# Local attention layers of a two-block network: keys copied by ScalarE, output products placed behind another tile's scores

## Chip, cores and metric

One core of a Trainium2 chip runs the whole kernel. Its engines are TensorE (PE, with weight loads shown as PEld), VectorE (DVE), ScalarE (ACT), GpSimd (POOL) and SyncE (SP, which issues transfers). The metric is device time in microseconds, median of several executions. Each engine works through its own list of instructions in a fixed order and waits on semaphores for the others.

## What is computed

Input: 4 sequences of 1024 tokens with 128 features. Block 0 is an attention of softmaxed features and a mixture of experts; block 1 begins with a windowed attention. Its last part, two local-attention layers with an MLP each, is the part that the change touches:

```python
def _layer(x, wqkv, qs, ksc, wo, lg, lb, w1, b1, w2, b2):
    h = shift_token(x)
    q, k, v = jnp.split(h @ wqkv, 3, axis=-1)
    q, k, v = (to_heads(q), to_heads(k), to_heads(v))      # 8 heads of 64
    q = l2norm(q) * qs
    k = l2norm(k) * ksc
    q, k = rotary_xpos(q, k)
    o = local_attention(q, k, v)     # windows of 64 tokens, each sees itself and the one before
    x = x + o.transpose(0, 2, 1, 3).reshape(b, n, INNER) @ wo
    h = shift_token(x)
    h = (h - mu) / jnp.sqrt(var + 1e-05) * lg + lb
    a, g = jnp.split(h @ w1 + b1, 2, axis=-1)
    x = x + (a * jax.nn.gelu(g, approximate=False)) @ w2 + b2
    return x

for l in range(DEPTH):               # DEPTH = 2
    x = _layer(x, ...)
```

All of it is in float32.

## The kernel before

The local layers work on tiles of 128 tokens: 2 layers x 4 sequences x 8 tiles = 64 tiles, counted by g. One loop (from line 1064) walks over g and issues in each iteration the steps of several tiles, so that their chains overlap:

- `scores(g)` (lines 875 to 896): 32 products on 64x64 parts of the array, in two banks of PSUM. VectorE adds the mask and takes the extreme of each row (L892, eight times).
- `project(g + 2, w)` (lines 647 to 676): the queries (w = 0) or keys (w = 1) of the tile two further on. PE multiplies (L653). ScalarE squares (L656, `sq`). VectorE multiplies with the cosine and sine tables (L658 `co`, L663 `si`) and sums the squares (L665, `ss`); `co` waits for `sq`. POOL adds `co` and `si` (L673), for the keys also raises the sums to the power -1/2 (L668, L669) and weights the keys with them (L675).
- `flip(g - 2, j)` (921 to 929): transposes half of the heads' probabilities, which ScalarE copies out (L928, `pt`).
- `over_sums(g - 1)` (907 to 919): VectorE takes the reciprocals of the sums (L912, `sm`); POOL weights half of the heads with them (L919), VectorE the other half (L919), or ScalarE in tiles 3 to 7 of the first sequence (L917, the `light` ones).
- `exps(g)` (898 to 905): eight exponentials on ScalarE (L904), each with its sum.
- `turn(g + 1, w)` (838 to 858): transposes the finished queries or keys. ScalarE copies the queries (L852, `qT`), VectorE the keys (L858, `kT`), which lie in one tile per sequence. In the first tiles the query turn takes twice the products (L849).
- `outputs(g - 3)` (931 to 944): 32 products of probabilities and values, on 128x64 parts of the array; ScalarE copies them out (L944, `os`).
- `values(g - 1)` (860 to 873): one product, a copy by ScalarE (L866, `vs`), and two transfers that SyncE issues and that shift the values by a window (`ve`).
- side steps, listed in `steps`: the output projection of 512 tokens (L951, L952) and the MLP: layernorm in (L972, L144 to L154) and out (L160, L161), gate with GELU (L986, L990), up (L995, L997), down (L1003, L1004).

What sets the order: PE's instructions run in the order in which the loop issues them (`manual_schedule` for PE alone). The lists of ScalarE, VectorE, POOL and SyncE are made by a scheduler when the program is built. It takes, of the instructions that its model holds to be ready, the one that stands first in program order. `issue_after(x)` adds a rule to this: what the block issues on the engine of `x` comes behind `x` in that engine's list. `over_sums` uses it: its VectorE instructions come behind the last `kept["copied"]`, the last copy of keys that had been issued. `kept` and `late` are one dictionary.

PSUM has 8 banks: two for scores, six for all else in the local layers, each given to the next tile when its reader is done.

Of the kernel before, what the change touches and what calls it, by code (L numbers as in the profile page):

```python
# [22 lines left out]
ALU = mybir.AluOpType  # L23
AX = mybir.AxisListType
PSUM = bass.MemoryType.PSUM

P = 128
# [21 lines left out]
def adaln_blocks(ctx: ExitStack, tc: tile.TileContext, a: dict, out: bass.AP):  # L49
    nc = tc.nc  # L50
    pe, act, dve, pool = nc.tensor, nc.scalar, nc.vector, nc.gpsimd
# [11 lines left out]
    def bc(ap, shape):  # L63

        return ap.unsqueeze(len(ap.shape)).to_broadcast(shape)
# [219 lines left out]
    with (  # L285
# [7 lines left out]
        kept = {}  # L293
# [306 lines left out]
    def const1(name, shape):  # L600
        return c1.tile(shape, F32, tag=name, name=name)

    wl = []
    for l in range(DEPTH):
        w = [const1(f"wqkv_{l}", [P, 3, HEADS * DH]), const1(f"wo_{l}", [P, 4, D]), const1(f"w1_{l}", [P, 2 * HID]), const1(f"w2_{l}", [P, 3, D])]
# [38 lines left out]
    late = {}  # L644
    pj = ctx.enter_context(tc.tile_pool(name="pj", bufs=3))

    def project(l, b, t, w, ps):


        nt = f"{l}_{b}_{t}_{w}"  # L650
        if w == 0:
            late[l, b, t, "ss"] = pj.tile([P, 2, HEADS], F32, tag="ss", name=f"ss_{nt}", bufs=4)
        pe.matmul(ps, lhsT=hs[l, b][:, t * P : (t + 1) * P], rhs=wl[l][0][:, w, :], start=True, stop=True)  # L653
        ph = ps.rearrange("p (h e) -> p h e", e=DH)
        sq = pj.tile([P, HEADS, DH], F32, tag="sq", name=f"sq_{nt}", bufs=2)
        act.activation(sq, ph, AF.Square)  # L656
        co = pj.tile([P, HEADS, DH], F32, tag=f"co{w}", name=f"co_{nt}")
        dve.tensor_tensor(co, ph, abs_[l][:, 0, t, w, :].unsqueeze(1).to_broadcast([P, HEADS, DH]), ALU.mult)  # L658
        si = pj.tile([P, HEADS, DH], F32, tag="si", name=f"si_{nt}", bufs=3)

        ex = bass.AP(tensor=ps.tensor, offset=ps.offset + 32, ap=[ps.ap[0], [DH, HEADS], [-32, 2], [1, 32]])
        sn = abs_[l][:, 1, t, w, :].rearrange("p (i e) -> p i e", i=2).unsqueeze(1).to_broadcast([P, HEADS, 2, 32])
        dve.tensor_tensor(si.rearrange("p h (i e) -> p h i e", i=2), ex, sn, ALU.mult)  # L663
        ss = late[l, b, t, "ss"]
        dve.tensor_reduce(ss[:, w, :], sq, AX.X, ALU.add)  # L665
        if w == 1:

            pool.tensor_scalar(ss, ss, 1.0e-24, None, ALU.max)  # L668
            pool.tensor_tensor(ss, ss, nhalf[:, 0:2].unsqueeze(2).to_broadcast([P, 2, HEADS]), ALU.pow)  # L669
        if w == 0 and light(l, b, t):  # L670
            late[l, b, t, "si"] = si
        else:
            pool.tensor_tensor(co, co, si, ALU.add)  # L673
        if w == 1:
            pool.tensor_tensor(co, co, bc(ss[:, 1, :], [P, HEADS, DH]), ALU.mult)  # L675
        late[l, b, t, "co", w] = co

    def light(l, b, t):

        return (l, b) == (0, 0) and t >= EARLY  # L680
# [5 lines left out]
    with (  # L686
# [80 lines left out]
        def project_out(b, k):  # L767
            s = slice(k * BLK, (k + 1) * BLK)
            yp = ps.tile([P, BLK], F32, tag="m", name=f"y1_{b}_{k}")
            pe.matmul(yp, lhsT=wout1, rhs=kept1[b, k, "os"], start=True, stop=True)  # L770
            dve.scalar_tensor_tensor(xT[b][:, s], yp, mods[1][:, 2, b : b + 1], xT[b][:, s], ALU.mult, ALU.add)
# [18 lines left out]
        def when(g, f, *args):  # L790
            if 0 <= g < NG8:
                f(*divmod(g, NT), *args)

        for g in range(-1, NG8 + 2):
            b, t = divmod(g, NT)
            ahead = 0 <= b and b + 1 < B
            if g == -1:
                weights(0, 0)
            when(g + 2, scores)
            when(g + 2, weights)  # L800
            if ahead and t in (2, 4):
                queries(b + 1, t // 2 - 1)
            for after, k, f in ((6, 0, tokens), (8, 0, normed), (11, 1, tokens), (13, 1, normed)):
                if (g - after) % NT == 0 and 0 <= (g - after) // NT < B - 1:
                    f((g - after) // NT, k, "h3")
            for at, k, f in ((1, 0, tokens), (3, 0, normed), (5, 1, tokens), (7, 1, normed)):
                if g == at:
                    f(B - 1, k, "h2")
            when(g - 1, back)
            when(g + 1, flip, (0, 1))  # L810
            when(g + 1, values)
            when(g, outputs)
            when(g + 1, flip, (2, 3))
            if t == 5 and 0 < b <= DEPTH:
                rotary(tab, abs_[b - 1], b - 1)
            if g % 4 == 1 and g > 4:
                project_out((g - 5) // NT, (g - 5) % NT // 4)
            if ahead and t in (3, 5):
                keys(b + 1, t // 2 - 1)

            for i, w in ((0, 0), (0, 1), (1, 0), (1, 1), (2, 0), (2, 1))[max(0, g - NG8 + 6) : max(0, g - NG8 + 7)]:
                project(0, 0, i, w, ps.tile([P, BLK], F32, tag="t", name=f"qk_0_0_{i}_{w}", bufs=2))
# [6 lines left out]
    with (  # L829
# [6 lines left out]
        kept = late  # L836

        def turn(l, b, t, w):
            nt = f"{l}_{b}_{t}_{w}"
            co = kept.pop((l, b, t, "co", w)).rearrange("p h e -> p (h e)")  # L840
            tp = pM.tile([P, 4, P], F32, tag="mid", name=f"qktr_{nt}")
            si = kept.pop((l, b, t, "si"), None) if w == 0 else None
            for i in range(4):
                if si is None:
                    pe.transpose(tp[:, i, :], co[:, i * P : (i + 1) * P], ident)  # L845
                else:

                    for j, x in enumerate((co, si.rearrange("p h e -> p (h e)"))):
                        pe.matmul(tp[:, i, :], lhsT=x[:, i * P : (i + 1) * P], rhs=ident, start=(j == 0), stop=(j == 1))  # L849
            if w == 0:  # L850
                kept[l, b, t, "q"] = wp.tile([P, 4, P], F32, tag="qT", name=f"qT_{nt}")
                act.copy(kept[l, b, t, "q"], tp)  # L852
                return
            if t == 0:

                kept[l, b, "k"] = wb.tile([P, 4, 64 + N], F32, tag="kT", name=f"kT_{nt}", bufs=1)
                pool.memset(kept[l, b, "k"][:, :, 0:64], 0.0)
            kept["copied"] = dve.tensor_copy(kept[l, b, "k"][:, :, 64 + t * P : 64 + (t + 1) * P], tp)  # L858

        def values(l, b, t):  # L860

# [45 lines left out]
        def over_sums(l, b, t):  # L907

            sm = kept.pop((l, b, t, "sm"))

            with tc.issue_after(kept["copied"].ins):
                dve.reciprocal(sm, sm)  # L912
                for j, eng in ((0, pool), (1, act if light(l, b, t) else dve)):
                    pr, _ = kept[l, b, t, "pr", j]
                    if eng is act:
                        for c in range(4):
                            act.activation(pr[:, c, :], pr[:, c, :], AF.Identity, scale=sm[:, j, c : c + 1])  # L917
                    else:
                        eng.tensor_tensor(pr, pr, bc(sm[:, j, :], [P, 4, P]), ALU.mult)  # L919
# [108 lines left out]
        for l in range(DEPTH):  # L1028
            for b in range(B):
                g = (l * B + b) * NT  # L1030
# [33 lines left out]
        for g in range(-1, tiles + 4):  # L1064
            side = steps.get(g, [])
            when(g, scores)
            when(g + 2, project_mid, 0)

            turns = {-1: (0, 1), 0: (2,), 1: ()}.get(g, (g + 1,))
            if 1 < g < NT - 1:  # L1070
                when(g + 1, turn, 0)
            when(g - 2, flip, 0)
            when(g - 1, over_sums)
            when(g + 2, project_mid, 1)
            when(g - 2, flip, 1)
            when(g, exps)
            for i in turns:
                if not 1 < g < NT - 1:
                    when(i, turn, 0)
                if i < EARLY and g < EARLY:  # L1080
                    when(i, turn, 1)
            when(g - 3, outputs)
            if g >= EARLY - 1:
                when(g + 1, turn, 1)
            for f, args in side[:1]:
                f(*args)

            for i in {0: (), 1: (0,)}.get(g, (g - 1,)):
                when(i, values)

            f0 = g - 7
            if f0 % 4 == 0 and 0 <= f0 < tiles - NT:
                lo = f0 % NT * P
                project_out(f0 // (B * NT), f0 // NT % B, lo, lo + BLK)
            for f, args in side[1:]:
                f(*args)
# [127 lines left out]
```

## Time and profile before

| | us |
|---|---|
| median of 3 runs | 1245.24 (1244.97 to 1251.0) |
| profiled execution | 1246.33 |
| its span | 1244.5 |
| local layers: first scores to the last ones' start | 581.3 to 1193.1 |

Work in the local layers, by line, over the whole run:

| line, engine, operation | times | mean ns |
|---|---|---|
| L904 ACT exponential | 512 | 403 |
| L656 ACT square | 128 | 586 |
| L928 ACT copy pt | 128 | 581 |
| L944 ACT copy os | 64 | 591 |
| L852 ACT copy qT | 64 | 576 |
| L858 DVE copy kT | 64 | 678 |
| L658, L663, L665 DVE | 128 each | 677, 678, 673 |
| L919 DVE | 59 | 808 |
| L912 DVE reciprocal | 64 | 188 |
| L673 POOL | 123 | 1280 |
| L669 POOL power | 64 | 2995 |
| L675 POOL | 64 | 1044 |
| L919 POOL | 64 | 1168 |

How to read it: durations are from an instruction's start to its end. Neighbours on one engine overlap by about a tenth of a microsecond, so a packed list advances faster than the sum of the durations; the chain of waits shows that advance. The profiled execution is 1.8 us longer than its span, which runs from the first to the last instruction.

### The profile page before, as it was taken

Reading aid. Unit: us, or ns where it says so; the run is one execution under the profiler, and the core shown is the slowest. Engines: PE = TensorE matmul, PEld = TensorE weight load, DVE = VectorE, ACT = ScalarE, POOL = GpSimd, SP = SyncE. Lnnn points to the kernel's source line nnn. Section 1 sums busy time; section 2 is a strip of 40 time slices with the busy share of each in tenths; the row PEclk is TensorE's granted clock in tenths of the full one; section 3 lists DMA queues with packets and bytes.
Section 4 is the critical chain, followed back from the end, with each engine's and each line's share of the span. In section 5 each row is a group of like instructions: output and inputs, shape, how many; then the busy total and the mean of one; then the engine's idle time right before and its main releaser. Section 6 shows DMA issues by size and latency. Waiting matters only on the chain.

```text
span 1244.5 us, 34772 instructions
## 1 busy us (share of the span) xinstructions
PE 1162.8 (93%) x13578; PEld 714.7 (57%) x13578; DVE 878.8 (71%) x2798; ACT 817.8 (66%) x2223; POOL 823.3 (66%) x813
## 2 busy tenths in 40 slices
PE   6789999999899999988898999999999999999998
PEld 5644453534476667755665556665555556565564
DVE  5556263452476667666878988898898888998864
ACT  3363373322577677766886788788877887788862
POOL 4436445746334445444889988888899889888840
PEclk8699999999999999999999999999999999999999
DMA  6040404021400000000112111111111111111110
GB/s 179 1 130 8 138 0 132 7 74 63 137 4 4 3 20 14 11 3 3 35 27 48 27 35 26 32 40 27 39 28 34 39 29 45 38 27 31 36 40 26
DMA packets 36136, 51.04 MB, mean 41 GB/s; under 512 B 5850, under 2 KB 17668, under 8 KB 35844
## 3 DMA queue, kind: packets, MB, share of 16 engines
q1 hardware_dynamic: 35540, 48.29, 14.1%
q8 instruction: 107, 1.75, 0.6%
q10 hardware_dynamic: 432, 0.53, 0.1%
q14 instruction: 57, 0.47, 0.1%
HBM read 26.52 MB, written 2.36 MB: 23 GB/s over the span
## 4 chain that ended last, share of the span: by engine, by line
PE 43%; DVE 27%; ACT 18%; POOL 7%; issue 5%; DMA 1%; POOLq 0%; ACTq 0%; SPq 0%; DVEq 0%
ACT pr L904 5%; PE h L489 4%; PE yp L951 4%; DVE pr L892 3%; DVE co L658 3%; PE s L885 3%; DVE si L663 3%; DVE ss L665 3%; PE ptr L735 3%; PE qk L653 3%; POOL u L494 2%; ACT sq L656 2%; PE s L261 2%; PE obank L752 2%; DVE ge L997 2%
## 5 line engine op out<-in xcount | busy, mean ns | idle before, releaser
L904 ACT ACTIVATE pr<-pr,mx 128x128 f32<-128x128 f32 x512 | 200.8, 403 | 88.2 <-DVE mx L892 88.1
L673 POOL TENSOR_TENSOR co<-co,si 128x512 f32<-128x512 f32 x123 | 156.7, 1280 | 79.5 <-DVE si L663 72.2
L669 POOL TENSOR_TENSOR ss<-ss,nhalf 128x16 f32<-128x16 f32 x64 | 191.7, 2995 | 5.3
L892 DVE CUSTOM_DVE_ANT_0 pr<-s,masks,ss 128x128 f32<-128x128 f32 x512 | 144.2, 342 | 42.4 <-PE s L885 42.0
L653 PE MATMUL qk<-wqkv,hs 128*128 128x512 f32 x256 | 137.7, 620 | 4.9 <-ACT pt L737 4.9
L494 POOL TENSOR_TENSOR u<-u,cw 128x512 f32<-128x512 f32 x64 | 81.1, 1271 | 74.4 <-ACT u L492 74.4
L489 PE MATMUL h<-hT,w 128*128 128x512 f32 x256 | 123.8, 605 | 4.0 <-DVE g L496 4.0
L496 DVE TENSOR_TENSOR g<-u,h 128x512 f32<-128x512 f32 x64 | 43.8, 686 | 114.9 <-POOL u L494 114.9
L279 DVE TENSOR_REDUCE mx<-s 128x4 f32<-128x448 f32 x128 | 73.5, 617 | 56.4 <-PE s L270 56.4
L658 DVE TENSOR_TENSOR co<-qk,ab 128x512 f32<-128x512 f32 x128 | 86.7, 677 | 26.0 <-ACT sq L656 26.0
L904 ACT ACTIVATION_READ_ACCUMULATOR pr<-pr,mx 128x1 f32 x512 | 101.7, 199 | 0.0
L492 ACT ACTIVATE u<-h 128x512 f32<-128x512 f32 x64 | 38.2, 598 | 93.2 <-PE h L489 85.7
L926 PEld LDWEIGHTS ptr<-ident,pr 128*128 128x128 f32 x512 | 63.5, 141 | 61.6 <-issue 54.8
L663 DVE TENSOR_TENSOR si<-qk,ab 128x512 f32<-128x512 f32 x128 | 86.8, 678 | 0.0
L489 PEld LDWEIGHTS h<-hT,w 128*128 128x128 f32 x256 | 48.3, 194 | 66.2 <-issue 51.0
L665 DVE TENSOR_REDUCE ss<-sq 128x8 f32<-128x512 f32 x128 | 86.2, 673 | 0.0
L656 ACT ACTIVATE sq<-qk 128x512 f32<-128x512 f32 x128 | 74.9, 586 | 14.8 <-PE qk L653 12.3
L845 PE MATMUL qktr<-ident,co 128*128 128x128 f32 x492 | 76.9, 280 | 6.6 <-POOL co L675 5.3
L885 PEld LDWEIGHTS s<-kT,qT 64*64 64x64 f32 x2048 | 56.8, 134 | 45.6 <-issue 22.1
L919 POOL TENSOR_TENSOR pr<-pr,sm 128x512 f32<-128x512 f32 x64 | 74.7, 1168 | 7.9 <-DVE sm L912 7.9
L885 PE MATMUL s<-kT,qT 64*64 64x128 f32 x2048 | 72.1, 277 | 7.6 <-DVE kT L858 6.1
L737 ACT COPY pt<-ptr 112x512 f32<-112x512 f32 x128 | 72.5, 612 | 8.6 <-PE ptr L735 8.6
(212 smaller groups left out, 2871.2 us busy)
## 6 DMA issues: line engine op xcount, KB each, us to landing
cw<-cd SPq DMA_DIRECT2D x128, 128.0 KB, 3.0
ve<-vs SPq DMA_DIRECT2D x120, 128.0 KB, 2.3
hs<-hT SPq DMA_DIRECT2D x16, 256.0 KB, 3.2
out<-out SPq DMA_DIRECT2D x7, 256.0 KB, 2.7
xin<-in_x SPq DMA_DIRECT2D x3, 512.0 KB, 6.1
w<-in_w SPq DMA_DIRECT2D x3, 512.0 KB, 5.0
wqkv<-in_wqkv SPq DMA_DIRECT2D x2, 768.0 KB, 5.3
ab<-in_tab SPq DMA_DIRECT2D x1, 1024.0 KB, 7.3
```

Source lines behind the costliest of these rows:

```text
L489: pe.matmul(h, lhsT=w[:, c * P : (c + 1) * P], rhs=hT[b][:, blk(k)], start=True, stop=True)
L494: pool.tensor_tensor(u, u, kept[b, k, "cw"][:, c, :], ALU.mult)
L653: pe.matmul(ps, lhsT=hs[l, b][:, t * P : (t + 1) * P], rhs=wl[l][0][:, w, :], start=True, stop=True)
L656: act.activation(sq, ph, AF.Square)
L658: dve.tensor_tensor(co, ph, abs_[l][:, 0, t, w, :].unsqueeze(1).to_broadcast([P, HEADS, DH]), ALU.mult)
L663: dve.tensor_tensor(si.rearrange("p h (i e) -> p h i e", i=2), ex, sn, ALU.mult)
L665: dve.tensor_reduce(ss[:, w, :], sq, AX.X, ALU.add)
L669: pool.tensor_tensor(ss, ss, nhalf[:, 0:2].unsqueeze(2).to_broadcast([P, 2, HEADS]), ALU.pow)
L673: pool.tensor_tensor(co, co, si, ALU.add)
L885: pe.matmul(S[j][qs, c, :], lhsT=q[rw, c, qs], rhs=k[rw, c, at : at + P], start=True, stop=True)
L892: dve.tensor_tensor_reduce(out=pr[:, c, :], in0=S[j][:, c, :], in1=mk[:, min(t, 1), :], scale=kept[l, b, t, "ss"][:, 0, h : h + 1], scalar ...
L904: act.activation(pr[:, c, :], pr[:, c, :], AF.Exp, bias=mx[:, j, c : c + 1], scale=-1.0, accum_out=sm[:, j, c : c + 1])
```

## The change

Three things are altered in the local layers.

1. `turn` for the keys: ScalarE copies `kT`, no longer VectorE.
2. `over_sums`: its VectorE instructions come behind the last sum of squares that had been issued (L665), no longer behind the last copy of keys. When `over_sums(g - 1)` is called, that is the sum of the query projection of tile g + 2 in the same iteration; the last copy of keys was that of the iteration before.
3. `outputs(g - 3)` is issued directly behind `scores(g)`, ahead of the query projection of tile g + 2. It stood between the turn of the queries and the turn of the keys.

No product, transfer or buffer is added or taken away.

```diff
@@ -662,7 +662,7 @@
         ss = late[l, b, t, "ss"]
-        dve.tensor_reduce(ss[:, w, :], sq, AX.X, ALU.add)
+        late["summed"] = dve.tensor_reduce(ss[:, w, :], sq, AX.X, ALU.add)
@@ -855,7 +855,7 @@
-            kept["copied"] = dve.tensor_copy(kept[l, b, "k"][:, :, 64 + t * P : 64 + (t + 1) * P], tp)
+            act.copy(kept[l, b, "k"][:, :, 64 + t * P : 64 + (t + 1) * P], tp)
@@ -908,7 +908,7 @@
-            with tc.issue_after(kept["copied"].ins):
+            with tc.issue_after(kept["summed"].ins):
                 dve.reciprocal(sm, sm)
@@ -1064,6 +1064,7 @@
             when(g, scores)
+            when(g - 3, outputs)
             when(g + 2, project_mid, 0)
@@ -1079,7 +1080,6 @@
                 if i < EARLY and g < EARLY:
                     when(i, turn, 1)
-            when(g - 3, outputs)
             if g >= EARLY - 1:
                 when(g + 1, turn, 1)
```

## The prediction

> **What bounds the kernel now.** I read the page first, then busy time by stretch, then the chain of waits inside one stretch, then the timeline of each engine.
>
> The page's busy line, and the same for one round of four tiles of the local layers (from the scores of one tile to those of the tile four later):
>
> ```profile
> PE 1162.8 (93%) x13578; PEld 714.7 (57%) x13578; DVE 878.8 (71%) x2798; ACT 817.8 (66%) x2223; POOL 823.3 (66%) x813
> ...
> 804.78:844.55 39.77, 39.49 (x383) 23.77 (x382) 34.27 (x119) 31.46 (x98) 35.01 (x29) 1.00 0.16 38
> ```
>
> The second line holds start and end, length, then busy PE, PEld, DVE, ACT, POOL, the clock and DMA. PE looks like the only bound: 39.49 of 39.77 us. The starts of the scores repeat this round from 744.62 to 1184.63 us, 440.0 us or 11 rounds; about one more lies before it. I call its four tiles A, B, C, D. In A the three GELUs run, in B the three "up" products and the next layernorm's input, in C "down", in D two output projections.
>
> The chain of waits says that the round is held by more than PE (start, duration, engine, tile, line):
>
> ```profile
> 806.44 0.55 ACT pr L904 x3
> ...
> 811.56 0.47 ACT qT L852
> 812.03 0.48 ACT os L944
> ...
> 817.93 0.49 ACT sq L656
> 818.42 0.02 issue
> 818.45 0.69 DVE co L658
> ...
> 822.12 0.60 DVE kT L858
> 822.72 1.97 DVE ge L997 x3
> ...
> 831.31 0.65 DVE pr L919
> ...
> 833.15 0.61 DVE kT L858
> 833.76 0.14 issue
> 833.89 1.10 PE s L885 x32
> ```
>
> One closed loop: scores of A (804.78), ScalarE without a gap for 12 us (exponentials, two table loads, GELUs) to the square of B, VectorE without a gap for 15.3 us to the turned keys of C, then PE through D to the next A (844.55). 13.67 + 15.3 + 0.14 + 10.66 = 39.77 us. PE alone would need 0.35 us less (833.54: it waits for kT, 0.23 us of gap and a slow first product). So two limits lie within 1% of each other, and an edit counts by what it does to both.
>
> PE's timeline in the same round:
>
> ```profile
> 853.92 1.10 PE L885 MATMUL s<-kT,qT 64*64 64x128 f32 x32
> 854.95 1.12 PE L653 MATMUL qk<-wqkv,hs 128*128 128x512 f32 x2
> ...
> 857.65 0.60 PE L845 MATMUL qktr<-ident,co 128*128 128x128 f32 x4
> 858.18 0.34 PE L940 MATMUL o<-pt,ve 128*64 128x64 f32 x4
> ...
> 859.26 0.66 PE L845 MATMUL qktr<-ident,co 128*128 128x128 f32 x4
> 859.75 1.02 PE L995 MATMUL a<-hn,w 128*128 128x512 f32 x2
> ```
>
> Four transposes run 0.109 us apart, 0.436 us; from the first turn to the outputs it is 0.53, from the second turn on 0.49. These are the prices of changing between products on parts of the array and on all of it.
>
> **Outputs behind the scores.** Record by record: scores to projection 0.199 us; last transpose to outputs 0.202 instead of 0.109; outputs to transpose 0.152, and the second transpose 0.055 late. After the change: scores to outputs, a; outputs to projection 0.152 (outputs to a 512-wide product, at 1202 us, shows that); the turns adjacent. Saved: 0.199 + 0.093 + 0.055 - a = 0.347 - a. No row has scores to outputs. Its ends are 0.007 (the step between independent 64x64 products) and 0.202 (whole array to parts); I take 0.152, from layernorm input (64x128) to scores, the one change from parts to parts. Saving 0.195 us a tile (0.145 to 0.340), 0.78 a round.
>
> TensorEngine Tiling in the Trainium skill ("Key Properties") says that changing the tiling mode, not just the tile, drains TensorE. Since 64*64 and 128*64 are different modes, that would put a at the upper end: 0.145 a tile. The 0.152 row agrees that parts to parts is not free.
>
> The step carries 32 products and one os copy, no DMA; its ve transfers were issued two iterations earlier and land in 2.3 us. What it moves back by about 1.0 us are both projections, both flips and the first turn. The second turn comes about 0.2 us earlier.
>
> **ScalarE takes kT.** A copy costs ScalarE 0.47 us in a packed queue (qT row), VectorE 0.60. But where? On ScalarE the path of the loop ends at the square of B. In front of that now stand kT of A (scores of B need it) and os of B: its outputs now come before B's projection in PE's order and in program order, and used to be copied after B's qT. 2 x 0.475 = +0.95 us. The 3.42 us for which ScalarE idles before A cover nothing of this, since A's exponentials wait there for VectorE.
>
> **The anchor.** sm and L919 of the tile before stood behind kT, at a time when VectorE often idled (2.06 us before B's scores). Now they stand behind the first reduce of the same iteration's projection, in front of si of the second. In B: less kT 0.60, plus sm 0.11 and L919 0.65, +0.16 to the end of B; +0.76 to B's second si. In C they stood there already (831.31).
>
> **Where that lands.** No longer in kT, but in the keys' weighting on POOL, which the second turn of the next tile needs:
>
> ```profile
> 831.36 1.50 POOL L919 TENSOR_TENSOR pr<-pr,sm 128x512 f32<-128x512 f32 x1
> 832.82 1.26 POOL L673 TENSOR_TENSOR co<-co,si 128x512 f32<-128x512 f32 x1
> ...
> 837.51 1.05 POOL L675 TENSOR_TENSOR co<-co,ss 128x512 f32<-128x512 f32 x1
> ```
>
> L675 of C ends at 838.55, D's second turn starts at 839.24: 0.69 us of slack. B's second si comes 0.95 + 0.76 = 1.71 later; POOL runs from there to L675 of C with 0.09 + 0.35 us of idle time to absorb it: +1.27 us, to 839.82. Second turn at 839.90, from it to the next scores 5.25 (5.31 less the 0.055): 845.15 against 844.55. **+0.60 us a round, x12 = +7.2 us.** PE's saving in A to C is not seen, as it waits in D. Ends of this term: -1.13 a round (0.78 + 0.35, nothing but PE binds), -13.6 us; and +0.83 with the contention below, +10.
>
> POOL's L919 takes 1.04 us alone and 1.50 where VectorE's L919 runs beside it (831.36). In B the two now come together, ahead of L673: POOL's free time moves to 823.54, past si at 823.23, and adds 0.23 a round. I leave it out of the middle value. SBUF — State Buffer ("Who interferes with whom") says that a VectorE instruction with two SBUF inputs and a GpSimd one that reads SBUF exclude each other for a whole instruction; that speaks against the new anchor, and by it the sum would be +0.83 a round.
>
> **The first tiles (609 to 645 us).** There ScalarE also weights four blocks per tile (L917, 1.28 us), now between its exponentials, whereas it did this in its idle time before them. From scores to kT: 1.66 + 8 x 0.39 + 2 x 0.48 + 2 x 0.47 + 0.47 + 0.48 + 1.28 + 0.59 + 0.1 = 9.6 us against a period of 8.57: +1.0 for each of three periods, +3.0. If L917 stays outside, kT no longer trails the second reduce and each gains 0.36 + 0.2: -1.7. Before the first scores kT queues behind two qT on ScalarE: +0.5 (0 to 1.0).
>
> **Sum:** 7.2 + 3.0 + 0.5 = 10.7 on a profiled execution of 1246.33 us (span 1244.5): 1257.0; the runs' median lies 1.09 below it: **1256**. Own range 1249 to 1263.
>
> **Rivals.**
> PE stays the only bound and takes its saving: 60 tiles x 0.195 = 11.7, plus 0.35 x 12 = 4.2: 1229 us (1221 to 1236). For it: PE 99% busy, and VectorE is relieved of 2.4 us a round. Against it: the closed loop above, in which ScalarE is gapless.
>
> The delays fit the slack. If os of B is copied behind B's square, 0.475 falls away and with it most of +0.60; the rest is the first tiles: 1247 us (1240 to 1250). Against it: program order puts it first, and it is ready while the GELUs still run.
>
> Much slower: ScalarE's queue gets kT of A behind the GELUs. From 812.03, 0.92 + 0.38 + 1.83 + 0.47 + 0.59 gives 816.2 where B's scores start at 814.15: 2.1 a round, x12 = 25: 1271 us. It decides if kT is planned later than the first GELU; PE's order (turn before gm) speaks against it. A milder form: a PSUM bank released by kT (v waits for kT 13 times already, 12.1 us) comes 1.8 us later.
>
> That the change doesn't do what it says: a at 0.202 and a planner that restores the old order leave 1245, part of the second rival.
>
> **Numbers.** Forecast 0.50, PE alone 0.20, fits the slack 0.17, much slower 0.13. I tell changes of over 0.5% (6.2 us: 1239 and 1251.5) from none. Slower: 0.9 of the forecast, all of the last, a little of the third: 0.59. Same: 0.19. Faster: 0.22, the second rival and the lower edge. The range 1236 to 1270 leaves out most of PE alone and the upper half of the last.
>
> **What would show it.** Right: PE's round shows gaps at the second turn of D, released by POOL L675; rounds of 40.2 to 40.6 us; ScalarE has os, kT in front of B's square; VectorE's sm and L919 stand inside each projection; scores to outputs near 0.15 us. Wrong: rounds of 38.6 us without a gap, or a gap at scores released by ScalarE's kT of over 1 us.

## The result and the profile after

The changed kernel takes 1264.51 us (median of 6 runs, 1261.66 to 1265.71), the kernel before 1245.58 us in the runs beside it (6 runs, 1244.14 to 1251.0). The ratio is 1.0142, with a 95% interval from 1.012 to 1.0165: slower. The forecast was 1256 us and slower. The direction was right, and the time lies inside the stated range of 1236 to 1270 us, but above the 1249 to 1263 us that were given to the forecast alone: the rise was 18.9 us where 10.7 were worked out. The profiled execution took 1264.45 us, with a span of 1262.7 us.

The page after, its busy line and its chain by engine:

```profile
PE 1163.9 (92%) x13578; PEld 718.0 (57%) x13578; DVE 849.8 (67%) x2734; ACT 850.1 (67%) x2287; POOL 824.6 (65%) x813
...
PE 37%; ACT 21%; DVE 20%; POOL 14%; issue 7%; DMA 1%; POOLq 0%; SPq 0%; ACTq 0%; DVEq 0%
```

64 copies have gone from VectorE to ScalarE, and PE is as busy as before. In the chain that ended last, POOL holds 14% of the span instead of 7%, ScalarE 21% instead of 18%, PE 37% instead of 43%. The time went into waiting for POOL and ScalarE.

One round of four tiles, busy time by stretch (start and end, length, busy PE, PEld, VectorE, ScalarE, POOL, clock and DMA):

```profile
812.84:853.49 40.65, 39.51 (x383) 23.91 (x383) 32.59 (x115) 33.55 (x102) 35.50 (x29) 1.00 0.16 37
```

PE works 39.51 us as it did before (39.49), but the round is 40.65 us long instead of 39.77. PE stood still for 1.14 us where it had stood still for 0.28. The granted clock is 1.00 in both.

The chain of waits inside this round (start, duration, engine, tile, line):

```profile
826.52 0.47 ACT os L944
826.99 0.51 ACT sq L656
...
829.40 0.11 DVE sm L912
...
830.07 0.64 DVE pr L919
...
837.58 1.05 POOL rv_m L153
...
840.92 1.25 POOL pr L919
...
842.38 1.27 POOL co L673
...
844.07 2.94 POOL ss L669
...
847.08 1.05 POOL co L675
...
848.17 0.66 PE qktr L845 x4
```

Read it downwards: ScalarE copies os of B and only then takes its square; VectorE has `sm` and L919 inside the projection; from 837.5 us on the chain runs over POOL, through the layernorm, L919 and the keys' weighting; its last instruction, L675 of C, lets the second turn of D start. POOL's own list is packed for longer than the chain says: from its first L673 of B (828.88 us, after 2.42 us of waiting for `si`) to the end of L675 of C (848.12 us) no gap in it is above 0.10 us. Two waits make 1.03 of PE's 1.14 us: 0.50 in B, for VectorE's L663, and 0.53 in D, for L675. Before, this loop closed at the scores of D behind kT on VectorE.

The extra 18.2 us of span come from these places. The start, up to the first scores of a local layer, is 0.9 us shorter; among the profiled executions of all kernels here it varies by 7 us (574.20 to 581.27), though block 0 is the same in all, so 0.9 us says nothing about the change. From there to the round pattern it is 171.22 us instead of 163.34: +7.9. The eleven rounds take 450.66 instead of 440.02: +10.6. The end gives +0.5.

### The profile page after: what moved, and what is told of

The parts are those of the page before. It is cut to its first block, busy times and chain, and to the rows that moved or that the text cites. A ratio compares the mean times of both kernels' runs of the same rounds, so it can differ in the third digit from the quotient of the medians.

```text
span 1262.7 us, 34784 instructions
## 1 busy us (share of the span) xinstructions
PE 1163.9 (92%) x13578; PEld 718.0 (57%) x13578; DVE 849.8 (67%) x2734; ACT 850.1 (67%) x2287; POOL 824.6 (65%) x813
## 4 chain that ended last, share of the span: by engine, by line
PE 37%; ACT 21%; DVE 20%; POOL 14%; issue 7%; DMA 1%; POOLq 0%; SPq 0%; ACTq 0%; DVEq 0%
ACT pr L904 5%; PE h L489 5%; PE yp L951 4%; POOL ss L669 4%; PE ptr L735 3%; DVE pr L892 2%; ACT sq L656 2%; PE s L261 2%; POOL u L494 2%; POOL co L673 2%; PE s L885 2%; ACT ge L990 2%; PE y L504 2%; DVE co L658 2%; DVE si L663 2%
## 5 line engine op out<-in xcount | busy, mean ns | idle before, releaser
L673 POOL TENSOR_TENSOR co<-co,si 128x512 f32<-128x512 f32 x123 | 156.1, 1269 | 91.6 <-DVE si L663 87.5
L669 POOL TENSOR_TENSOR ss<-ss,nhalf 128x16 f32<-128x16 f32 x64 | 187.1, 2924 | 5.3
L919 POOL TENSOR_TENSOR pr<-pr,sm 128x512 f32<-128x512 f32 x64 | 90.2, 1410 | 16.0 <-DVE sm L912 15.9
L663 DVE TENSOR_TENSOR si<-qk,ab 128x512 f32<-128x512 f32 x128 | 86.9, 679 | 0.0
L665 DVE TENSOR_REDUCE ss<-sq 128x8 f32<-128x512 f32 x128 | 86.1, 672 | 0.0
L845 PE MATMUL qktr<-ident,co 128*128 128x128 f32 x492 | 68.2, 275 | 17.9 <-POOL co L675 16.6
```

## The experiments

No kernel leaves any of the work out. A round is the distance from the scores of one tile A to those of the next; "first tiles" is the period between scores at 609 to 645 us; "eleven rounds" is the stretch that took 440.02 us before. Line numbers in a run's views are those of its own kernel and move by the lines added to it.

| run | median us | ratio to before, 95% | first tiles | eleven rounds | one round |
|---|---|---|---|---|---|
| before | 1245.58 | | 8.57 | 440.02 | 39.77 |
| the whole change | 1264.51 | 1.0142 (1.012 to 1.0165) | 9.47 | 450.66 | 40.65 |
| kt_alone | 1248.22 | 1.0041 (1.0022 to 1.006) | 8.26 | 444.65 | 40.25 |
| anchor_alone | 1256.01 | 1.0094 (1.0065 to 1.0123) | 8.57 | 450.76 | 40.75 |
| outputs_alone | 1253.84 | 1.0079 (1.0055 to 1.0102) | 9.90 | 444.29 | 40.21 |
| no_anchor | 1250.18 | 1.0049 (1.003 to 1.0068) | 8.88 | 443.93 | 40.09 |
| no_outputs | 1256.56 | 1.0111 (1.0083 to 1.0139) | 9.43 | 448.50 | 40.57 |
| no_kt | 1259.55 | 1.0131 (1.0107 to 1.0155) | 8.68 | 452.60 | 40.93 |
| os_late | 1258.27 | 1.0119 (1.0097 to 1.0142) | 9.42 | 446.78 | 40.39 |
| kt_some | 1238.69 | 0.997 (0.9956 to 0.9985) | 8.26 | 437.68 | 39.52 |
| kt_some_early | 1240.95 | 0.9958 (0.9935 to 0.9981) | 8.26 | 438.46 | 39.60 |
| kt_some_dve | 1236.9 | 0.9907 (0.9873 to 0.994) | 8.26 | 432.59 | 39.15 |
| all3 | 1231.72 | 0.9874 (0.9834 to 0.9914) | 8.26 | 429.72 | 38.81 |

The median of before was 1243.51, 1242.5 and 1246.76 us beside the three groups of runs, so the ratios are what to compare.

### Each part by itself

**kt_alone** moves only the copy of kT. VectorE's `sm` and L919 then have no copy to stand behind, so they stand behind the second projection's sum, next to their old place.

```diff
-        dve.tensor_reduce(ss[:, w, :], sq, AX.X, ALU.add)
+        of = dve.tensor_reduce(ss[:, w, :], sq, AX.X, ALU.add)
+        if w == 1:
+            late["summed"] = of
...
-            kept["copied"] = dve.tensor_copy(kept[l, b, "k"][:, :, 64 + t * P : 64 + (t + 1) * P], tp)
+            act.copy(kept[l, b, "k"][:, :, 64 + t * P : 64 + (t + 1) * P], tp)
...
-            with tc.issue_after(kept["copied"].ins):
+            with tc.issue_after(kept["summed"].ins):
```

> Only the copy of the keys moves to ScalarE; the weights' normalization stays where it was (its anchor is the keys' own sum of squares of the iteration before), outputs stay between the two turns. Loop theory (the time is set by the closed path ScalarE of A and B, VectorE of B and C, POOL of C, PE of D): +0.48 on ScalarE before B's square, but this order of ScalarE has the square in front of the table load and the first exponential (-1.7), so VectorE starts B as soon as its scores are masked, 0.8 us earlier, and sheds two key copies: rounds of 39.0 to 39.4 us, 1237 us (1232 to 1242). Rival, ScalarE's load (30 us more work on the engine that gates the round): about 1262, as in the whole change.

Measured: 1.0041, slower, a miss. The first tiles did gain (8.26 instead of 8.57), the rounds lost 0.48 us. The chain of its round:

```profile
822.38 1.35 ACT pr L906 x7
823.73 0.48 ACT qT L854
...
824.25 1.13 PE v L866 x2
...
825.77 1.03 PE s L887 x32
```

The expectation had the square of B ahead of the second table load. In this chain kT of A is copied at 813.20 us, and the square of B comes at 819.12, behind the load (817.33) and two exponentials. So ScalarE reaches qT of B late; the value product needs the PSUM bank that this copy frees, and the scores of C stand behind it on PE. ScalarE alone sets this stretch.

**anchor_alone** moves only `sm` and L919 to the sum last issued.

```diff
-        dve.tensor_reduce(ss[:, w, :], sq, AX.X, ALU.add)
+        late["summed"] = dve.tensor_reduce(ss[:, w, :], sq, AX.X, ALU.add)
...
-            with tc.issue_after(kept["copied"].ins):
+            with tc.issue_after(kept["summed"].ins):
```

> Only the normalization moves behind the first reduce. Loop theory: VectorE +0.76 in B, but the square of B comes 1.2 us earlier in this order of ScalarE, which gives 0.8 back: rounds of 39.7 to 40.0 us; the first tiles lose about 1.3 us each, as ScalarE's L917 comes between its exponentials and delays the keys' square: 1250 us (1246 to 1255). ScalarE's load: 1245, nothing moved to it.

Measured: 1.0094, more than expected. Here kT is still VectorE's and now has both instructions ahead of it. The chain at the end of its VectorE stretch:

```profile
835.22 0.61 DVE kT L858
...
835.97 1.10 PE s L885 x32
```

It is the old loop, made longer: +0.98 us a round. The square of B comes 13.16 us behind the scores of A, as before (13.15), so the 1.2 us that it was expected to come earlier are not there. From it to the end of kT of C it is 16.54 us instead of 15.83, +0.71: `sm` and L919 (0.11 and 0.64) now stand ahead of kT of B. Another 0.25 lies in D (10.91 us instead of 10.66), where the output projection starts late. The first tiles are unchanged (8.57).

**outputs_alone** moves only the outputs.

```diff
             when(g, scores)
+            when(g - 3, outputs)
...
-            when(g - 3, outputs)
```

> Only the outputs move behind the scores. Loop theory: os of B now stands in front of B's square on ScalarE, +0.48; PE saves 0.15 us in D: rounds of 40.1 us, 1249 us (1245 to 1253). Rival, changing array shape pays (0.148 us x 60 tiles): 1237. ScalarE's load: 1245 or the saving.

Measured: 1.0079, somewhat slower than expected. In its chain os of B (823.91 us) stands directly ahead of the square of B (824.38), and the stretch on VectorE behind it ends with kT of C (839.67), as before but later: +0.44 us a round. In the first tiles the period is 9.90 instead of 8.57; there os now stands among the exponentials, but the chain of that stretch was not followed.

### The whole change without one part

**no_anchor**, against the changed kernel:

```diff
-        late["summed"] = dve.tensor_reduce(ss[:, w, :], sq, AX.X, ALU.add)
+        of = dve.tensor_reduce(ss[:, w, :], sq, AX.X, ALU.add)
+        if w == 1:
+            late["summed"] = of
```

> The whole change with the normalization left at its old place (anchored on the keys' sum of squares of the iteration before). Loop theory: ScalarE +0.95 and one exponential (+0.39) before B's square, VectorE -0.6; keys' weighting of C 0.9 later, of which 0.69 is slack: rounds of 39.9 to 40.1 us, POOL's L919 back at 1.04 us, first tiles without their 0.9 us: 1247 us (1242 to 1251). ScalarE's load: 1262.

**no_outputs**, against the changed kernel:

```diff
             when(g, scores)
-            when(g - 3, outputs)
...
+            when(g - 3, outputs)
             if g >= EARLY - 1:
```

> Keys copied by ScalarE and the normalization moved, outputs at their old place. Loop theory, from the chain of the run with the copy alone (rounds of 40.3 us, ended by ScalarE's B, 0.55 us later than before): the keys' weighting of C comes another 0.76 + 0.23 - 0.44 later, which the second turn of D just takes: rounds of 40.3 to 40.5 us, 1251 us (1247 to 1256). Rival, the three edits' costs add up (4.7 + 12.5 us of the two single runs): 1261.

**no_kt**, against the changed kernel:

```diff
-            act.copy(kept[l, b, "k"][:, :, 64 + t * P : 64 + (t + 1) * P], tp)
+            kept["copied"] = dve.tensor_copy(kept[l, b, "k"][:, :, 64 + t * P : 64 + (t + 1) * P], tp)
```

> Outputs and normalization moved, VectorE keeps the copy of the keys. Loop theory: the chain of the outputs-alone run (rounds of 40.2 us, VectorE from B's square to the keys of C) gets 0.76 us longer in B: rounds of 41.0 us, slower than the whole change in the rounds, 1263 us (1258 to 1268): the copy on ScalarE is then a part that helps beside the other two. Rival, ScalarE's extra copies are what costs: near the outputs-alone run, 1254.

Measured: 1.0049, 1.0111 and 1.0131. The first and the last came as expected. no_outputs is a miss: 40.57 us a round is a little above what was expected, and over the whole run 1.11% is nearer to the two single costs added up (1.35%) than to the 0.5% expected. In the rounds they do not add up: 8.5 us, where the two alone cost 4.6 and 10.7. Taking the anchor back is worth most: about two thirds of the loss goes, in the rounds 6.7 us of 10.6. Taking the outputs back is worth 2.2 us in the rounds. Taking the copy back makes the rounds slower still (452.60 against 450.66): once the anchor is where the change put it, kT is better off on ScalarE. Over the whole run the two can't be told apart, as their intervals overlap. The parts don't add up. Alone they cost 0.4, 0.9 and 0.8%, together 1.4%.

**os_late** is the whole change with the os copy issued at its old place; only the products of the outputs are early.

```diff
-            act.copy(kept[l, b, t // 4, "os"][:, :, i * P : (i + 1) * P], o)
+            kept[l, b, t, "o"] = o
+
+        def outputs_copy(l, b, t):
+            i = t % 4
+            act.copy(kept[l, b, t // 4, "os"][:, :, i * P : (i + 1) * P], kept.pop((l, b, t, "o")))
...
+            when(g - 3, outputs_copy)
             if g >= EARLY - 1:
```

> The whole change, but the copy of the outputs out of PSUM is issued at the old place of the outputs; the products stay behind the scores. Loop theory: os leaves the stretch of ScalarE ahead of B's square, -0.48 us a round, on the path that ends with the keys' weighting of C: rounds of 40.2 us, 1259 us (1255 to 1263). If the outputs cost through PE's order (later projections) or a bank: 1264, or more as a bank is held longer.

Measured: 1.0119. From D to the next A it is 10.92 us instead of 11.26, but A to C is 0.08 longer, so a round gains 0.26. The step "os of B ahead of the square of B" is confirmed: the square comes 13.62 us behind the scores of A instead of 14.15, which is the whole copy. Only about half of it reaches the round, because another wait then decides: PE's first "up" product in B waits 0.52 us for VectorE's L663 (828.80 us), and the second turn of D no longer waits for POOL in any gap that the trace lists. Over the whole run the intervals of os_late and of the whole change overlap.

### A version that is faster

If the loop through ScalarE and VectorE is the reason, the copies should go where the engine has time in that tile, not to one engine throughout. **kt_some** gives ScalarE the copy of kT only in the first tiles and in iterations C and D; VectorE keeps it in A and B.

```diff
+        of = dve.tensor_reduce(ss[:, w, :], sq, AX.X, ALU.add)
+        if w == 1:
+            late["copied"] = of
...
+    def quiet(g):
+
+        return g < 12 or g % 4 in (2, 3)
...
+            to = kept[l, b, "k"][:, :, 64 + t * P : 64 + (t + 1) * P]
+            if quiet((l * B + b) * NT + t - 1):
+                act.copy(to, tp)
+            else:
+                kept["copied"] = dve.tensor_copy(to, tp)
```

> The kernel before, with the keys copied by ScalarE only where no GELU is near (tiles C and D of a round, and the first 12 iterations), by VectorE in A and B. Loop theory: VectorE no longer ends the loop with the keys of C, ScalarE's A and B carry no more than before: A to C as before (19.4 us), C to D 9.37 instead of 9.67: rounds of 39.5 us, first tiles 8.26 us each: 1240 us (1236 to 1244). Rival, any copy on ScalarE costs: between 1245 and 1249.

Measured: 0.997 (0.9956 to 0.9985), a small gain, in the first tiles and in the wait of C's scores for kT.

**kt_some_early** adds the early outputs in A, C and D of the rounds, not in B.

```diff
+            early = g >= 12 and g % 4 != 1
+            if early:
+                when(g - 3, outputs)
             when(g + 2, project_mid, 0)
...
-            when(g - 3, outputs)
+            if not early:
+                when(g - 3, outputs)
```

> The run with the keys on ScalarE in C and D alone, and the outputs directly behind the scores in A, C and D from iteration 12 on, in B at the old place. Loop theory: A to C stays at 19.5 us (ScalarE of A, VectorE of B), C and D each save the 0.148 us of array shapes: rounds of 39.2 us, 1235 us (1232 to 1239). Rival, outputs behind the scores cost by themselves (projections 1 us later): 1240 or more.

Measured: 0.9958, not told from kt_some (the intervals overlap), a miss; the eleven rounds take 438.46 instead of 437.68. A and C are 0.16 and 0.15 us shorter, B and D 0.15 and 0.22 longer. What PE saves it waits for again: the chain of its round still runs over ScalarE in A and VectorE in B, and goes on over POOL to the second turn of D, which waits 0.16 us for the keys' weighting.

**kt_some_dve** leaves the outputs where they were and has VectorE copy os and the values in A, the tile of the GELUs.

```diff
+            g = (l * B + b) * NT + t + 1
+            (dve.tensor_copy if g >= 12 and g % 4 == 0 else act.copy)(v, ps.rearrange("p (h e) -> p h e", e=DH))
...
+            g = (l * B + b) * NT + t + 3
+            (dve.tensor_copy if g >= 12 and g % 4 == 0 else act.copy)(to, o)
```

> The run with the keys on ScalarE in C and D alone, and in A VectorE copies os and vs, which it can do in the 2 us in which it waits for B's scores. Loop theory: ScalarE is 0.95 us shorter ahead of B's square, of which VectorE's masking of B leaves 0.79 to gain, until PE alone sets A to C (19.1 us): rounds of 39.2 us, 1234 us (1230 to 1238). Rival, VectorE's load costs: 1239 or more.

Measured: 0.9907. ScalarE reaches the square of B earlier, B falls from 10.12 to 9.76 us, the round to 39.15.

**all3** is kt_some with both additions.

```diff
+                act.copy(to, tp)
...
+            (dve.tensor_copy if g >= 12 and g % 4 == 0 else act.copy)(v, ps.rearrange("p (h e) -> p h e", e=DH))
...
+            (dve.tensor_copy if g >= 12 and g % 4 == 0 else act.copy)(to, o)
...
+            early = g >= 12 and g % 4 != 1
```

> Keys on ScalarE in C and D, os and vs of A on VectorE, outputs behind the scores in A, C and D. Loop theory: PE alone sets the round: 9.22 + 9.76 + 9.22 + 10.51 = 38.7 us, 1230 us (1226 to 1235). If a new wait takes over (banks of PSUM, POOL): 1235 or more.

Measured: 0.9874 (0.9834 to 0.9914), faster than both kernels. The chain of its round is PE from end to end:

```profile
by line: PE qk L653 19.5%; PE s L896 11.7%; PE o L951 11.0%; PE yp L964 9.8%; PE qktr L851 9.5%; PE ptr L937 8.9%; PE v L874 8.7%; PE ym L1016 6.6%; PE gm L999 6.6%; PE a L1008 6.6%; PE out_m L160 1.1%; PE in_m L985 1.0%
```

With nothing but PE in it, the early outputs are worth what they save on PE: 0.15 us in A (9.36 to 9.21) and in C (9.37 to 9.22), 0.04 in D, where the second turn still waits a little for POOL. Early outputs give this only together with a relieved ScalarE; added to kt_some they gave nothing. This is read in the rounds (432.59 to 429.72 us for eleven): over the whole run the intervals of all3 and kt_some_dve overlap.

## Why the prediction was right, and its size wrong

**The closed loop, and where it lands: right.** The rise was put at the second turn of D behind L675 of C. The trace after has this chain, and its steps agree in time. From the scores of A to the square of B: 13.15 us before, 0.95 more expected, 14.15 measured (826.99 less 812.84). To the end of the second `si` of B: 18.45 expected (823.23 less 804.78), 18.46 measured (831.30 less 812.84). The round, 40.65 us, is just above the 40.2 to 40.6 that were named as the sign of being right.

**The contention, left out of the middle value: wrong, and the largest miss in the round.** The step said that POOL's L919 beside VectorE's L919 "adds 0.23 a round. I leave it out of the middle value." In the rounds before, all POOL instructions of L919 (times, shortest, median and longest, in ns):

```profile
L919 POOL TENSOR_TENSOR pr<-pr,sm x44: 1037/1042/1507, 751.8 to 1177.9; 128x512 f32<-128x512 f32 x44
```

and after:

```profile
L919 POOL TENSOR_TENSOR pr<-pr,sm x44: 1484/1488/1496, 759.6 to 1199.5; 128x512 f32<-128x512 f32 x44
```

Before, the long ones are the 11 of 44 that overlap VectorE's L919; after, all 44 overlap it. The new anchor brings them together in each tile, since both now follow the first `si` of the same projection: POOL's L919 stands behind its first L673, VectorE's behind `ss`, `sm` and `co`. In B of the round above:

```profile
829.98 0.72 DVE L919 TENSOR_TENSOR pr<-pr,sm 128x512 f32<-128x512 f32 x1
830.11 1.49 POOL L919 TENSOR_TENSOR pr<-pr,sm 128x512 f32<-128x512 f32 x1
...
831.56 1.27 POOL L673 TENSOR_TENSOR co<-co,si 128x512 f32<-128x512 f32 x1
```

The second L673 starts when POOL has finished L919, 0.26 us behind the end of the second `si` (831.30), where before it started 0.07 behind it (821.60 and 821.53). The second turn of D was expected 35.12 us behind the scores of A (839.90 less 804.78) and came after 35.33 (848.17 less 812.84): 0.21 late, which is about the term that had been left out. No run takes this overlap alone away.

SBUF — State Buffer in the Trainium skill ("Who interferes with whom"), by which the two exclude each other, spoke against the new anchor with reason. The rows agree with it on both sides: VectorE's L919 is long too, where POOL's L673 still runs when it starts. In the rounds before and after:

```profile
L919 DVE TENSOR_TENSOR pr<-pr,sm x44: 691/722/1423, 751.6 to 1173.0; 128x512 f32<-128x512 f32 x44
...
L919 DVE TENSOR_TENSOR pr<-pr,sm x44: 722/1002/1570, 759.0 to 1199.3; 128x512 f32<-128x512 f32 x44
```

After, it takes 0.72 us where L673 has 0.18 us left (829.98), 1.09 with 0.54 left (840.42) and 1.56 with 1.01 left (807.94). The prediction had no price for this side, but in B, on the chain, it is the short case. How long each engine stands still within the 0.59 us of overlap, the records do not show; POOL's lasts 0.45 longer.

**From the second turn to the next scores: a little too short.** 5.25 us expected, 5.32 measured (853.49 less 848.17). The step had taken off 0.055 for turns that stand adjacent. In D they are adjacent in PE's list only: PE waits between them, and the four transposes behind the wait take as long as they took behind the outputs (0.66 us in both records; 0.60 for those that directly follow other transposes, at 847.04). So 0.60 + 0.21 + 0.07 = 0.88 us a round, which is the measured 40.65 less 39.77. All of the 0.28 by which the round was mis-sized is in these two terms. Over eleven rounds it is 9.7 us; the other 0.9 of the 10.6 lie in the last four rounds, which also write out results and are 1.11 us longer each; why was not followed.

**The first part: half the size.** +3.0 for the first tiles was near (9.47 us against 9.6 worked out; three periods of +0.9 are +2.7), and by the step that was named: ScalarE's L917 (615.33 us) stands among the exponentials, ahead of kT (617.85), for which the next scores wait. What was not seen is the rest of the +7.9 before the rounds. 3.1 us of it is one step at 674 to 689 us, 15.11 us from scores to scores where before had 11.98. The chain after, there:

```profile
677.87 2.93 POOL ss L669
...
680.87 1.44 POOL co L675
...
682.36 0.66 PE qktr L845 x4
...
683.46 1.62 PE v L864 x2
685.07 4.37 PE yp L951 x8
```

and the stretch behind the turn (columns as above):

```profile
682.40:686.00 3.60, 3.60 (x12) 2.04 (x13) 0.20 (x1) 1.89 (x4) 3.44 (x4) 0.64 0.02 5
```

Two things make the 3.1 us. PE waits 2.68 us for POOL ahead of this turn, where it waited 1.25 before: +1.4, the same wait as in the rounds, but one in which POOL had no idle time to give. Behind it the granted clock is low (0.64 in the row above, 0.88 in the 3.50 us after it, 1.00 in the same step before): the value product and the output projection advance in 1.62 and 4.37 us instead of 0.86 and 3.43, +1.7. Whether the longer wait brought the clock down is not shown, as no run changes the wait alone. The prediction had no term for the clock; it had counted rounds, and had not followed the tiles that lead into them one by one. The remaining 2.1 us (7.9 less 2.7 less 3.1), of which 1.8 in the tiles that start at 635 to 670 us before, have not been traced to single waits.

**The step from scores to outputs: the wrong row.** The term a was taken at 0.152 us, between 0.007 and 0.202. Start to start it measured 0.199 to 0.200 in 61 tiles, the upper end. From outputs to the projection it is 0.152 as assumed. So the saving on PE is 0.347 - 0.199 = 0.148 us a tile, not 0.195. This cost the forecast nothing, since PE waits in the round anyway; it did matter to the first rival, and all3 shows 0.15 in the two tiles where PE alone decides. The row that was chosen stands behind products 64 wide, but the scores are 128 wide. By the width of the product in front, the rows agree: 0.152 us behind 64 (layernorm input to scores, outputs to projection), 0.199 to 0.203 behind 128 (scores to outputs or projection, transposes to outputs), 0.52 behind 512 (output projection to scores). Without a change of shape, products 128 and 512 wide follow each other after 0.109 and 0.429. So a change costs about 0.09 us on top of the last product's own step; this is an estimate from these rows, and no run varies the width alone.

The Trainium skill's TensorEngine Tiling (Array Packing), section "Key Properties", says that a change of tiling mode drains TensorE, and 64*64 to 128*64 is one. The rows agree that it is not free. But the 0.152 row is such a change too, so the rule did not decide between the two values. PE's records at the new place:

```profile
833.01 1.10 PE L885 MATMUL s<-kT,qT 64*64 64x128 f32 x32
834.05 0.34 PE L940 MATMUL o<-pt,ve 128*64 128x64 f32 x4
...
835.13 1.13 PE L653 MATMUL qk<-wqkv,hs 128*128 128x512 f32 x2
```

**The rivals.** PE alone as the bound, the fast one, was not this kernel; but all3 shows that it is there once the copies are shared out: 39.15 us a round without early outputs, where "less 0.35" had made it 39.42, and 38.81 with them. The 0.35 was too small, since it counted the wait in C alone: there C falls by 0.30 us (9.67 to 9.37), but B too, by 0.32 (10.08 to 9.76). The slow one, kT behind the GELUs, is refuted: kT of A is copied at 820.61, ahead of the GELUs at 822.41. Its milder form, a PSUM bank released later, is in the trace: the value product of the same round waits 0.50 us for VectorE's L663, which frees its bank:

```profile
831.36 1.13 PE L864 MATMUL v<-wqkv,hs 128*128 128x512 f32 x2 [0.50 <-DVE si L663]
```

This gap does not lie on the chain that closes the round, since the second turn of D waits longer still, by 0.53 us. It is the next limit, though: in os_late and no_outputs a wait of 0.52 us for the same L663 is the only one listed for PE in the round. In kt_alone the same kind of wait, behind ScalarE's qT, does decide.

**Sum.** 10.7 us expected and 18.2 measured in span: the rounds gave +10.6 where +7.2 stood (for one round more), the part before them and the start +7.0 where +3.5 stood, the end +0.5. The +0.5 for kT ahead of the first scores is lost in the scatter of the start and stays open.

## What to carry to other kernels

Where two limits lay within 1% of each other, what a copy cost on a less busy engine was decided by what stands behind it in that engine's list in each tile, and not by the engine's busy share: the same copy cost 0.4% in all tiles and gained 0.3% in the tiles where ScalarE had room. A cost that has a row in the trace and only needs two instructions to come together belongs in the middle value as soon as the edit makes both follow the same instruction. A steady pattern does not price the tiles that lead into it; go through those one by one.

## What was not expected of the hardware

- VectorE's L919 and POOL's L919 side by side cost POOL 0.45 us each time (1488 ns against 1042, medians). VectorE pays too where POOL's L673 is still at work: up to 1570 ns instead of 722.
- In these rows a change of tiling adds about 0.09 us to the last product's own step, whichever shapes change: 0.199 us instead of 0.109 behind 128-wide products, 0.52 instead of 0.429 behind 512-wide ones.
- A group of four transposes starts as slowly behind a wait as behind a change of tiling: 0.66 us instead of 0.60, at a granted clock of 1.00.
